# The second image joins the shared silu group, and the planner gets a new table of ties

## The chip, the cores and the metric

The kernel runs on one core of a Trainium2 chip. The metric is the device time of one execution in microseconds (us). An execution with a profiler attached also gives a trace of every instruction; times inside it are counted from the first instruction of the program. The engines are named PE (matrix multiply), PEld (its weight loads), DVE (vector), ACT (scalar activations), POOL (GpSimd) and SP (the queue that issues the DMAs).

## The reference, cut to what matters

The input is eight images of 384 channels and 1024 positions in float32. For every image a selective-scan mixer is applied and added to the input; for the first five images a quantised feed-forward network follows.

```python
t = layernorm(layernorm_over_channels(x))        # per position
xm, z = split(t @ in_proj_w.T)                   # 768 + 768 channels
xc = silu(causal_conv3(xm) + conv_b)
dt, Bm, Cm = split(xc @ x_proj_w.T)              # 24 + 16 + 16
dt = softplus(dt @ dt_proj_w.T + dt_proj_b)
h[l] = exp(dt[l] * A) * h[l-1] + dt[l] * xc[l] * Bm[l]   # 16 states a channel
y = (sum over states of h[l] * Cm[l] + xc * D) * silu(z)
x = x + mlp(y @ out_proj_w.T)                    # gelu between two layers, then its residual
# images 0 to 4 only: t = t + ffn(layernorm(t)), signs as weights, clipped by a maximum over the image
```

## The kernel before, in words

**Tiling.** An image is worked on in two halves of 512 positions (`T`). A tile is 128 partitions wide; 768 channels are six such groups, kept in three pieces of two groups each (`PER` = 2). Four kinds of work exist for an image `b`:

- the *front* (`s1`, L697): two norms, the products `p_in` and `p_z` with `in_proj_w` (six groups each, three 128x128 weights a group; each float32 multiply appears as two matmul records in the trace), the convolution on DVE (L763), silu of `xc`, the product `p_dbc` (L797), a fold and a row sum `p_all` (L807), the products `p_dt` (L828), softplus of `dt`, and the product `dtx` = dt·xc on POOL (L844). Results go to DRAM: `xc_d`, `z_d`, `dt_d`, `dtx_d` and `rows_d`;
- the *scan* (`s2`, L862, and `scan`, L875): twelve units an image. Each loads its rows again, spread out over states, and runs through exp on ACT (`da`, L584), multiplications on POOL (L992), the scan instruction on DVE (L1017) and sums on PE into `py` (L956). Image 0 and image 7 are scanned half by half, the others whole;
- the *back* (`s3`, L1051): the products `p_out`, `p_h` and `p_o` with gelu between them;
- the *feed-forward* (`ffn`, L1255) of images 0 to 4, with the products `p_y`.

**Order.** No loop order of the program is the order of the instructions. `Plan.add` (L218) writes down every operation with its engine, an assumed cost and what it reads and writes. `Plan.run` (L265) then plays these out on an assumed clock and emits the instructions of each engine in the order in which the planner starts them. On the chip each engine keeps that order and waits for semaphores. When an engine has several operations that could start, `choose` (L291) narrows the set and `rank` (L316) sorts it: scans of images first by class, fronts (lanes 1, 4, 11, 14) next, everything else after that. Within a class the order is the order of writing down, `op.prio[2]`, moved by up to 16 places either way by a hash, `turned` (L100). The seed of this hash comes from the table `TURNS` (L93): entry n is used while the planner's clock is between 100·n and 100·(n+1) us. Bits above 65535 of an entry change a rule for that stretch, such as fronts later or scans first on DVE. Past the end of the table the seed is 0, which leaves the written order. The planner also emits a small multiply called `spare` (L478), of which nothing is used, where it expects PE to be idle for over 0.7 us.

**Buffers.** Tiles come from rings, which hand out buffers in the order of writing down within a lane. Fronts use the ring `front` (six pieces) and the weight ring `w_f` (four). The front of image 1 alone runs in lane 11 and takes other rings: `hid` (nine pieces) for `xc`, `dt` and `z`, and `w_b` (three weights); both serve the back and the feed-forward later. PSUM has three buffers `mm` and two `da`.

**The activation tables.** An ACT operation carries the name of the table that it needs (`silu`, `softplus`, `gelu`, `exp`, or none). `choose` stays with the present table, where it is not exp, while an operation of it can start. `in_place` (L713) makes a group of silu or softplus, one instruction per piece: the first instruction waits for all the pieces of the group, the rest follow it.

```python
        def in_place(func, table, *ts):                                   # L713
            parts = [t[k] for t in ts for k in range(KD)]
            for p, piece in enumerate(piece for t in ts for piece in t.pieces):
                mine = parts[p * PER : (p + 1) * PER]
                self.act(..., r=parts if p == 0 else mine, w=mine, table=table)
...
            z = gate(half, t) if b in JOINT else None                     # L783
            in_place(AF.Silu, "silu", *([xc, z] if z else [xc]))
            by_pair("xc", half, xc)
            if z:
                by_pair("z", half, z)
...
            if not z:                                                     # L857, after softplus, dtx and dt
                z = gate(half, t)
                in_place(AF.Silu, "silu", z)
                by_pair("z", half, z)
```

`gate` (L733) writes down the six weight loads, the six `p_z` groups and their copies; `by_pair` (L704) the stores to DRAM.

Of the kernel before, what the change touches and what calls it, by code (L numbers as in the profile page):

```python
# [34 lines left out]
B, C, L = 8, 384, 1024  # L35
# [36 lines left out]
MM = 0.859  # L72
MODE = 0.097
SWITCH = 0.22
JOINT = range(2, B)
BATCH = 2
SIGNAL = 0.05
DRAIN = 0.2
# [12 lines left out]
STRETCH, REACH = 100, 16  # L91
LATE_FRONTS, DVE_SCANS, POOL_SCANS, ACT_STAGES = 1 << 16, 1 << 17, 1 << 18, 1 << 19
TURNS = (  # L93
    59965, 29935, 54697, 25830, 41556, 52704, 5806, 54013, 24204, 552223,
    25982, 47623, 34875, 16007, 24111, 42172, 43083, 15421, 638691, 11540,
    33479, 220645, 233617, 13861, 59336, 49176, 14182, 227647, 59245, 317456,
)


# [318 lines left out]
class Layer:  # L418
# [278 lines left out]
    def s1(self, b):  # L697
# [15 lines left out]
# [4 lines that stand above are left out]
                self.act(lambda piece=piece: piece.real, lambda piece=piece: piece.real, func,  # L717
                         c_act(PER * T), r=parts if p == 0 else mine, w=mine, table=table)
# [14 lines left out]
        def gate(half, t):  # L733
            z = self.split(r_z, KD, "z")
            for m in range(KD):
                w = self.weights(r_w, KC, a["in_proj_w"][KD + m])
                pm = self.mm3(w, t, [t[k] for k in range(KC)], [z.pieces[m // PER]], "p_z")
                self.affine(
                    lambda m=m, z=z: z.at(m), lambda pm=pm: pm.real, [pm], [z[m]]
                )  # L740
            return z

        for half, cols in enumerate(HALVES):
# [38 lines left out]
            all_m = [xc[m] for m in range(KD)]  # L782
            z = gate(half, t) if b in JOINT else None  # L783
            in_place(AF.Silu, "silu", *([xc, z] if z else [xc]))
# [647 lines left out]
```

## Time and profile before

| What | Value |
|---|---|
| time, median of 3 runs | 3134.88 us (3129.45 to 3136.87) |
| time of the profiled execution | 3132.08 us |
| its span, first to last instruction | 3130.3 us |
| mean granted PE clock | 0.993 |
| PE busy | 3049.4 us (97%), of it 58.6 us in `spare` |
| POOL busy | 2802.1 us (90%) |
| DVE busy | 2599.5 us (83%) |
| ACT busy | 2019.1 us (65%), of it 273.3 us in 213 table loads |
| DMA | 751.76 MB, 240 GB/s on average |

Busy times are unions of the instructions of an engine. A matmul record is longer (597 ns) than the distance from one to the next, since they are pipelined; so the idle time of PE says more than its busy time does. Line numbers are those of the kernel before. Many operations are recorded by a helper, so L568 (all large products) and L584 (all table functions) are told apart by the tiles' names.

### The profile page before, as it was taken

To read this page: it belongs to the slowest core of one execution; us is meant where nothing else is said; L and a number is where in the kernel's file an instruction comes from. 1 tells how busy PE (TensorE), PEld (TensorE's weight loads), DVE (VectorE), ACT (ScalarE), POOL (GpSimd) and SP (SyncE) were. 2 spreads that over 40 slices of the span, in tenths; PEclk is the share of its full clock that TensorE was granted. 3 is DMA by queue.
4 is the path that set the end of the run, shared out by engine and by line. 5 is a ranking of instruction groups with operands and counts; after the bars stand their busy time and mean duration, and the time that the engine had idled before them with its cause. 6 is when DMAs were issued, how large, how long until landed. Compare 5 with 4: busy or idle time off the path is not lost.

```text
span 3130.3 us, 32297 instructions
## 1 busy us (share of the span) xinstructions
PE 3049.4 (97%) x10202; PEld 1243.8 (40%) x10202; DVE 2599.5 (83%) x2053; ACT 2019.1 (65%) x2406; POOL 2802.1 (90%) x1095
## 2 busy tenths in 40 slices
PE   9899999999999999999999999999999999999999
PEld 4334333333333444434343334343334444333334
DVE  4787888999987889878799888898788988798880
ACT  4887787776576566667666665666745556666562
POOL 2889888999999998999989998999999999999880
PEclk9999999999999999999999999999999999999999
DMA  7999778777787667777679675886877756756442
GB/s 231 305 312 314 241 255 282 272 251 254 256 318 241 207 202 259 280 263 259 202 256 319 206 231 194 298 276 211 269 250 229 238 187 220 243 187 211 155 152 73
DMA packets 348969, 751.76 MB, mean 240 GB/s; under 512 B 36480, under 2 KB 113792, under 8 KB 339584
## 3 DMA queue, kind: packets, MB, share of 16 engines
q1 hardware_dynamic: 348368, 749.61, 71.9%
q8 instruction: 82, 1.34, 0.2%
q14 instruction: 87, 0.71, 0.1%
q10 hardware_dynamic: 432, 0.09, 0.0%
HBM read 569.21 MB, written 180.36 MB: 239 GB/s over the span
## 4 chain that ended last, share of the span: by engine, by line
PE 53%; DVE 6%; DMA 5%; ACT 5%; POOL 4%; issue 2%; SPq 0%; DVEq 0%; POOLq 0%; ACTq 0%
PE p_y L568 16%; PE p_o L568 11%; PE p_h L568 9%; PE py L956 7%; PE p_out L568 5%; POOL u L992 3%; DVE u L1017 2%; PE p_in L568 2%; DVE da L1017 2%; PE p_z L568 2%; ACT da L584 1%; ACT L584 1%; DMA w_b<-in_mlp_w 1%; DMA w<-in_mlp_w 1%; DMA w_n<-bin_w 1%
## 5 line engine op out<-in xcount | busy, mean ns | idle before, releaser
L584 ACT ACTIVATE da<-dt_r,a_neg 128x1024 f32<-128x1024 f32 (+1 forms) x960 | 898.2, 944 | 559.4 <-DVE u L1017 292.1
L992 POOL TENSOR_TENSOR u<-dtx_r,bc 128x2048 f32<-128x2048 f32 (+1 forms) x360 | 1186.4, 3311 | 75.7 <-PE py L956 38.8
L1017 DVE TENSOR_TENSOR_SCAN u<-da,u 128x1024 f32<-128x1024 f32 (+1 forms) x436 | 871.2, 2009 | 165.7 <-POOL u L992 77.7
L992 POOL TENSOR_TENSOR u<-u,bc 128x2048 f32<-128x2048 f32 (+1 forms) x274 | 900.0, 3290 | 74.4 <-DVE u L1017 68.0
L568 PE MATMUL p_h<-t,w_b 128*128 128x512 f32 x1152 | 513.1, 597 | 10.7 <-DMA w_b<-in_mlp_w 5.0
L568 PE MATMUL p_o<-g,w 128*128 128x512 f32 x1152 | 512.3, 597 | 7.5 <-DMA w<-in_mlp_w 5.7
L1017 DVE TENSOR_TENSOR_SCAN da<-da,dtx_r 128x1024 f32<-128x1024 f32 (+1 forms) x192 | 380.4, 2014 | 51.1 <-POOL dtx_r L992 31.4
L992 POOL TENSOR_TENSOR dtx_r<-dtx_r,bc 128x2048 f32<-128x2048 f32 (+1 forms) x120 | 397.0, 3312 | 1.8
L568 PEld LDWEIGHTS p_o<-g,w 128*128 128x128 f32 x1152 | 214.6, 190 | 299.7 <-issue 271.1
L568 PE MATMUL p_y<-gf,w_n 128*128 128x512 f32 x720 | 323.5, 601 | 9.3 <-DMA w_n<-bin_w 6.0
L568 PEld LDWEIGHTS p_h<-t,w_b 128*128 128x128 f32 x1152 | 213.9, 190 | 298.1 <-issue 259.8
L568 PE MATMUL p_y<-tn,w_b 128*128 128x512 f32 x720 | 318.9, 597 | 3.2 <-DVE rstd L685 2.5
L956 PE MATMUL py<-u,fold 128*32 128x512 f32 x2304 | 303.2, 625 | 0.0
L1017 DVE TENSOR_TENSOR_SCAN da<-da,u 128x1024 f32<-128x1024 f32 (+1 forms) x140 | 280.8, 2037 | 11.7 <-ACT da L584 10.8
L584 ACT ACT_TABLE_LOAD x213 | 273.3, 1283 | 5.5 <-DMA dt_r<-dt_d 1.8
L568 PE MATMUL p_out<-yg,w 128*128 128x512 f32 x552 | 245.5, 596 | 2.1 <-DMA w<-in_out_proj_w 1.3
L568 PE MATMUL p_in<-t,w_f 128*128 128x512 f32 x504 | 230.6, 606 | 12.6 <-issue 5.2
L568 PE MATMUL p_z<-t,w_f 128*128 128x512 f32 x504 | 227.1, 599 | 2.0 <-issue 1.0
L568 PEld LDWEIGHTS p_y<-gf,w_n 128*128 128x128 f32 x720 | 134.1, 191 | 196.0 <-issue 173.4
L568 PEld LDWEIGHTS p_y<-tn,w_b 128*128 128x128 f32 x720 | 134.4, 190 | 184.5 <-issue 167.0
L1037 DVE TENSOR_TENSOR dtx_r<-da,bc 128x1024 f32<-128x1024 f32 x144 | 170.8, 1214 | 0.1
L599 ACT ACTIVATE g<-p_h,v_vecs 128x512 f32<-128x512 f32 x159 | 107.5, 678 | 89.9 <-PE p_h L568 89.4
(131 smaller groups left out, 3152.4 us busy)
## 6 DMA issues: line engine op xcount, KB each, us to landing
dtx_r<-dtx_d SPq DMA_DIRECT2D x72, 1024.0 KB, 5.9
dt_r<-dt_d SPq DMA_DIRECT2D x144, 512.0 KB, 5.1
w_b<-in_mlp_w SPq DMA_DIRECT2D x192, 192.0 KB, 3.5
w<-in_mlp_w SPq DMA_DIRECT2D x96, 384.0 KB, 3.4
w_f<-in_in_proj_w SPq DMA_DIRECT2D x168, 192.0 KB, 4.4
y_d<-y SPq DMA_DIRECT2D x120, 256.0 KB, 4.9
gf<-y_d SPq DMA_DIRECT2D x60, 512.0 KB, 6.3
xc_d<-xc SPq DMA_DIRECT2D x48, 512.0 KB, 6.1
```

Source lines behind the costliest of these rows:

```text
L568: self.nc.tensor.matmul(p.real, w.real[:, w0 + k, :], t.at(k0 + k), start=start and k == 0, stop=stop and k == n - 1,)
L584: lambda: self.nc.scalar.activation(out(), in_(), func, **{k: v() if callable(v) else v for k, v in kw.items()}),
L599: nc.scalar.activation(out(), in_(), AF.Identity, bias=bias, scale=scale)
L956: nc.tensor.matmul(py.real[g * DQ : (g + 1) * DQ, :], self.fold, hc, start=False, stop=(q == NQUAD - 1), skip_group_check=True,)
L992: nc.gpsimd.tensor_mul(u.real[:, x], t.real[:, x], row.real.unsqueeze(2).to_broadcast([P, n, 2]))
L1017: da=da, in_u=in_u: nc.vector.tensor_tensor_scan(to(i), da.real[:, i, :], in_u(i), state.real[:, col : col + 1] if half else 0.0, ALU.mult ...
L1037: nc.vector.tensor_mul(u.real[:, 0, :, t], da.real[:, 0, :], cq.real)
```

## The change

`JOINT` is the set of images whose front makes `z` before the silu of `xc`, so that one group of six silu instructions serves both. It was images 2 to 7 and becomes images 1 to 7. For both halves of image 1, the six weight loads, the six `p_z` groups with their copies, three silu instructions and three stores of `z` are written down ahead of `p_dbc`, and no longer after `dt`. The rings of image 1 (`hid` and `w_b`) stay. The table `TURNS` is another one throughout, with 31 entries for 30, and with other entries that carry rule bits; so the order among equals can differ in any part of the kernel. No operation is added or left out.

```diff
-JOINT = range(2, B)
+JOINT = range(1, B)
...
 TURNS = (
-    59965, 29935, 54697, 25830, 41556, 52704, 5806, 54013, 24204, 552223,
-    25982, 47623, 34875, 16007, 24111, 42172, 43083, 15421, 638691, 11540,
-    33479, 220645, 233617, 13861, 59336, 49176, 14182, 227647, 59245, 317456,
+    49843, 0, 14285, 9398, 319468, 15448, 107859, 44413, 48398, 70601,
+    17958, 35163, 36370, 107033, 276429, 33905, 16527, 550033, 11076, 25285,
+    28427, 1340, 188371, 35681, 649167, 22066, 0, 682652, 12089, 9636,
+    42095,
 )
```

## The prediction

> **What bounds the kernel.** I read the page first, then busy times by stretch, then the timelines of PE and ACT where PE is not full. By stretch (busy us and instruction count per engine, granted clock, DMA share, GB/s):
>
> ```profile
> 0.00:100.00 100.00, 88.47 (x353) 44.15 (x354) 45.99 (x71) 52.03 (x70) 36.86 (x35) 0.97 0.75 251
> 100.00:320.00 220.00, 207.25 (x773) 87.32 (x772) 177.13 (x182) 185.55 (x277) 193.36 (x135) 0.95 0.92 304
> 320.00:3046.00 2726.00, 2673.06 (x8880) 1077.39 (x8879) 2368.45 (x1792) 1765.87 (x2041) 2571.91 (x926) 1.00 0.72 240
> 3046.00:3131.00 85.00, 80.59 (x200) 34.97 (x198) 7.92 (x10) 15.70 (x20) 0.00 (x0) 1.00 0.25 75
> ```
>
> The columns after the length are PE, PEld, DVE, ACT, POOL. From 320 us on PE is 98% busy and POOL 94%. Part of PE's time is `spare`, which is disguised idling: the same view for that tile gives 11.22, 22.46, 24.29 and 0.60 us (sum 58.57). So PE lacks real work for 100-88.5+11.2 = 22.8 us, then 220-207.25+22.46 = 35.2 us, 77.2 us, and about 4 us. Every other microsecond is product work that the change leaves alone. **The end is set by PE: its fixed work plus these holes.** The second bound is the scan, seen in the end of PE's timeline:
>
> ```profile
> 3051.00 1.11 PE L956 MATMUL py<-u,fold 128*32 128x512 f32 x8
> 3051.93 1.08 PE L956 MATMUL py<-dtx_r,fold 128*32 128x512 f32 x8
> 3052.93 4.56 PE L568 MATMUL p_out<-yg,w 128*128 128x512 f32 x10
> ...
> 3064.63 31.06 PE L568 MATMUL p_h<-t,w_b 128*128 128x512 f32 x72
> 3095.53 31.06 PE L568 MATMUL p_o<-g,w 128*128 128x512 f32 x72
> ```
>
> The last sums of the scan end at 3053, and PE then has about 8.7 us of `p_out` that does not need them (3052.93 to 3061.62). So the scan has some 8 us to spare at the end, and no more: **to end earlier by much, both must be quicker; to end later, one is enough.**
>
> The change acts in 95 to 330 us, where image 1's front lies. There ACT shows 26 table loads. This is `z` of image 1, half 1, as a separate group, and the joint group of image 2, half 0:
>
> ```profile
> 262.32 1.28 ACT L584 ACT_TABLE_LOAD   x1
> 263.61 1.06 ACT L584 ACTIVATE z<-z 128x1024 f32<-128x1024 f32 x1
> ...
> 267.54 1.28 ACT L584 ACT_TABLE_LOAD   x1
> ```
>
> ```profile
> 283.09 1.28 ACT L584 ACT_TABLE_LOAD   x1
> 284.38 1.06 ACT L584 ACTIVATE xc<-xc 128x1024 f32<-128x1024 f32 x1
> 285.46 1.28 ACT L584 ACT_TABLE_LOAD   x1
> ...
> 292.11 1.28 ACT L584 ACT_TABLE_LOAD   x1
> 293.40 2.00 ACT L584 ACTIVATE z<-z 128x1024 f32<-128x1024 f32 x2
> ```
>
> The joint group is **torn in two**: one silu, then back to exp, then the rest with a second pair of loads. Over the whole trace 29 loads lead to silu; 8 belong to the four halves of images 0 and 1, so 21 serve the 12 joint halves, 1.75 each against 2 for a half with two groups. And PE pays for the wait:
>
> ```profile
> 291.81 5.16 PE L478 MATMUL spare<-small 128*128 128x256 f32 x22
> 296.89 1.07 PE L797 MATMUL p_dbc<-xc,w_f 128*64 128x512 f32 x2
> ```
>
> **What the Trainium skill says.** "ScalarE: Activation LUTs", section "What ACT_TABLE_LOAD costs", gives about 1283 ns for a load and about 1380 ns of drain. The trace agrees on the first (1283 mean, 213 loads) and not on the second: the copy before 262.32 ends at 262.30, and silu starts at 263.61. I price a load at 1.29 us. The same page's "Table sets: the hidden batching unit" says to batch by set; the torn groups show that a wider group saves less than a pair of loads here. "Perfetto Trace Analysis", section "Identifying the Most-Contended Engine", warns that matmul busy time misleads; the 58.6 us of `spare` inside 97% agree. "TensorE: Matmul & The Clock Gate", Part 1, says that PE's clock halves after idle windows; 0.95 in 100 to 320 against 1.00 after it (about 11 us) agrees.
>
> **The change part by part.** The sum is against the profiled 3132.08 us (span 3130.3 plus 1.8 around it), 2.8 below the median of 3134.88; I move the sum to the median.
>
> *Table loads.* Two separate groups become one in each of two halves: at best four loads, 4 x 1.29 = 5.2 us of ACT; at worst none, if both are torn; at the 1.75 of the others, one load, 1.3 us. This comes back only where someone waits for ACT: in 95 to 330 us DVE waits 17.0+10.8 us for `da` and POOL 6.6 us for `dt`, 34.4 of 235 us, 15%. I take -0.2 us, with ends -5.2 and 0.
>
> *`p_z` ahead of `p_dbc`.* Per half, 36 records (six per 2.8 us in the timeline, hence 15.6 us of PE), six copies (0.58 us on ACT or 0.69 on DVE), three silu (1.05 us), six weight DMAs (192 KB) and three `z_d` stores move forward. On SP's queue they pass the loads for `p_dbc` and `p_dt`, one `rows_d`, three `dtx_d` and three `dt_d` issues; all these, softplus on ACT, and the three `dtx` products on POOL (2.37 us each) come about 15.6+3.1 = 19 us later. In POOL's order the multiplications of image 0's scan stand behind `dtx`; a late `dtx` would hold them. What covers the delay of the data: image 1's scan begins at its first `py` of about 546 us (the 13th unit), while its `dt` is stored by 240. If that cover were gone, 19 us per half would count. The `hid` ring takes 3+3+3 = 9 pieces, exactly its size, as before: cost 0, at worst one wait for a store to land (6.6 us median).
>
> *PE's waits in this stretch.* `p_z` of image 1 now waits for its weights (1.59 and 2.47 us), since `w_b` hands them out behind those of `p_dt`; that goes: -4.1. In exchange both `p_dbc` come behind a joint group, like image 2's (5.2 us of `spare`), where half 1 now has 5.0 us and half 0 none: +5.4. Net +1.3. Lower end: neither hole forms, -9.1. Upper end: the whole stretch of 281 to 297 us around image 2's group, 13.1 us of `spare`, comes twice in place of the 5.0: +21.2.
>
> *The table of ties.* It removes no work, and no row of before shows its effect. What the order among equals can do is read from images with equal work: in the stretches 899, 1269, 1639 and 1995 (each to the next, the last to 2365) PE lacks work for 4.8, 8.1, 3.1 and 6.7 us, but in 2365 to 2696 for 331-327.45+19.39 = 22.9, with a hole around the maximum of a feed-forward (2502 to 2516, filled with `spare`). One such hole more or less is about 18 us. I take 0, with ends -20 and +25; the gain is the shorter side because of the scan.
>
> *Sum:* -0.2+1.3+0 = +1.1 on 3134.9, so 3136.
>
> **The rivals.**
> 1. *Little moves* (chance 0.38): the sum above, 3136, own range 3122 to 3150. For it: the gain lies on ACT, which is 65% busy, and 300 us ahead of need.
> 2. *Slower* (0.32): the joint stage of image 1 repeats image 2's hole. PE has nothing else in hand at 100 to 320, since no back or feed-forward is ready before 360. 2 x 13.1 - 5.0 = 21.2, so 3156. It decides from the point where `spare` and idle of PE in 100 to 320 exceed 35.2 us and the scan doesn't gain the difference. Against it: image 0's second half can fill in, as `p_in` does at 97 to 113.
> 3. *Faster* (0.26): the new order has no hole like that at 2502 (-18) and all four loads go (-5.2): 3112. For it: such holes are 20 us of 139. Against it: the scan would have to end over 8 us earlier too, with POOL at 94%.
> 4. *The change doesn't do what it says* (0.04): both groups of image 1 are torn, 213 loads stay, and the order changes only among idle neighbours: 3135.
>
> **How the numbers follow.** A measurement of this kernel tells 0.3%, 9.4 us, from no change: 3125.5 and 3144.3 are the borders. Rival 1 gives 0.05 faster, 0.22 same, 0.11 slower; 2 gives 0.32 slower; 3 gives 0.26 faster; 4 gives 0.01, 0.02, 0.01. Together 0.32, 0.24, 0.44. Cases of both signs hold most of the chance, so the range reaches to both: from 3104 (rival 3 with most of its ends) to 3170 (rival 2 with 14 us of the table's upper end). The predicted time is rival 1's.
>
> **What would show it.** Right: 209 to 213 table loads; `p_z<-t,w_b` ahead of `p_dbc<-xc,w_b` in both halves, with no wait for weights; `spare` of 17 to 28 us in 100 to 320; the thirteenth `py` within 10 us of 546; PE idle after 320 within 15 us of 77. Wrong: a change of over 10 us that is already there when image 1's scan starts (rival 2's place), or one that arises in a single image after 900 us (the table, with either sign), or a last scan sum that comes over 8 us late relative to PE's end.

## The result, and the profile after

The changed kernel takes 3143.01 us (median of 10 runs, 3139.17 to 3150.51), the kernel before 3133.16 us beside it (10 runs, 3127.42 to 3139.77). The ratio is 1.0031, with a 95% interval of 1.0019 to 1.0042: slower by some 10 us. The profiled execution took 3139.18 us, with a span of 3137.3, which is 7.0 more than the one of before; the stretches below are to be held against these 7.0. All line numbers of the changed kernel are higher by one.

Busy times by stretch, the changed kernel (after the length: PE, PEld, DVE, ACT, POOL, each with its count, then granted clock, DMA share, GB/s):

```profile
0.00:100.00 100.00, 91.58 (x352) 44.71 (x353) 46.44 (x67) 47.56 (x68) 37.09 (x35) 0.98 0.72 238
100.00:320.00 220.00, 199.46 (x711) 80.04 (x709) 180.62 (x192) 189.31 (x271) 189.93 (x135) 0.91 0.91 299
320.00:2240.00 1920.00, 1894.28 (x6413) 768.74 (x6414) 1700.77 (x1272) 1264.04 (x1441) 1805.42 (x610) 1.00 0.76 254
2240.00:3046.00 806.00, 783.72 (x2530) 321.54 (x2529) 671.87 (x517) 478.35 (x584) 752.88 (x306) 1.00 0.64 207
```

The same view of the kernel before, for the last two of these stretches:

```profile
320.00:2240.00 1920.00, 1882.57 (x6339) 755.32 (x6338) 1688.01 (x1259) 1279.44 (x1449) 1808.34 (x613) 1.00 0.75 252
2240.00:3046.00 806.00, 790.49 (x2542) 322.07 (x2541) 680.44 (x534) 486.43 (x593) 763.57 (x314) 1.00 0.66 211
```

Add the time of `spare` (after: 13.19, 8.67, 18.64 and 26.98 us; before: 11.22, 22.46, 3.70 and 20.59) and PE lacks real work as follows:

| Stretch (us) | before | after | difference |
|---|---|---|---|
| 0 to 100 | 22.8 | 21.6 | -1.2 |
| 100 to 320 | 35.2 | 29.2 | -6.0 |
| 320 to 2240 | 41.1 | 44.4 | +3.3 |
| 2240 to 3046 | 36.1 | 49.3 | **+13.2** |

The four rows sum to +9.3, and from 3046 us to the end both kernels lack some 4.5 us. PE's busy time without `spare` is 2.4 us shorter after (2988.4 against 2990.8), which leaves about the 7.0.

In 100 to 320 the granted clock fell from 0.95 to 0.91 at the same time, which gives back about 0.04 x 220 = 9 us at most; so image 1's front, where the joint group acts, comes out near level. The largest loss is in the last 800 us, where image 1 is long done. The scan shows when it arises. An image is scanned in twelve units, and a unit starts with ACT's `py<-xr,v_vecs`. The first unit of an image starts, before and after, at 545.8 and 538.8 us (image 1), 899.1 and 901.5 (image 2), 1994.9 and 1992.2 (image 5), 2364.6 and 2363.7 (image 6), 2695.7 and 2709.9 (image 7). **At the start of image 6 the two kernels are level; image 6 takes 346 us in place of 331.**

Level is a balance. Image 1's own scan takes 362.7 us in place of 353.3, which uses up its earlier start. The profiles of the experiments that keep the first 22 entries agree (363 to 365 us with the group and the early entries of the change, 353 with those of before); the cause is open. The earlier start itself is less sure: a profile shows one execution, and in six profiles with the same order up to here image 1's scan starts between 534.7 and 546.5 us.

The end of PE's timeline, the changed kernel:

```profile
3061.81 1.12 PE L957 MATMUL py<-u,fold 128*32 128x512 f32 x8
3062.75 1.08 PE L957 MATMUL py<-dtx_r,fold 128*32 128x512 f32 x8
3063.76 5.42 PE L569 MATMUL p_out<-yg,w_n 128*128 128x512 f32 x12
...
3071.57 31.17 PE L569 MATMUL p_h<-t,w_b 128*128 128x512 f32 x72 [0.24 <-ACT t L598]
3102.58 31.06 PE L569 MATMUL p_o<-g,w 128*128 128x512 f32 x72
```

The last sums of the scan end at 3063.8 against 3053.0, 10.8 us late. After them PE had 8.7 us of independent `p_out` before and 5.3 us now; the closing `p_h` begins at 3071.57 against 3064.63, 6.9 us late, and the span is 7.0 us longer. What POOL did meanwhile, in image 6's stretch and from there to the last sum, before and then after:

```profile
2364.00:2696.00 332.00, 328.45 (x1105) 138.57 (x1104) 301.06 (x207) 188.46 (x199) 321.56 (x95) 1.00 0.67 217
2696.00:3053.00 357.00, 348.88 (x1077) 138.33 (x1075) 291.52 (x268) 223.59 (x316) 323.75 (x183) 1.00 0.59 184
```

```profile
2364.00:2710.00 346.00, 340.32 (x1149) 146.26 (x1148) 299.80 (x210) 188.52 (x203) 333.86 (x105) 1.00 0.67 219
2710.00:3064.00 354.00, 339.17 (x1048) 133.34 (x1047) 294.19 (x265) 213.92 (x304) 312.10 (x173) 1.00 0.56 174
```

In image 6's stretch POOL is idle for 10.4 us before and for 12.1 after. Of the 14 us more, 12.3 are more work, and 10.4 of these are the end of image 4's feed-forward (the clip of `y` and six additions), which the kernel before runs after image 6, at 2701 to 2721 us. So image 6's longer scan is for the most part work that was moved into it. After it POOL has 11.7 us less to do, and the stretch is only 3 us shorter: POOL is idle for 33.3 us before and for 41.9 after. Both stretches together have 10.3 us more of idle time, about the delay of the scan. It is a fitting reading, and not shown, that this work costs time in image 6, where POOL is 97% busy, and hides after it, where POOL is 91% busy in the kernel before: no run moved these operations alone, and e8 below speaks against POOL's work alone as the bound of image 6.

The growth of POOL's idle time is in waits for a scan of DVE, and after image 6 (5.2 us before and 6.4 after in image 6's stretch). From there to 3046 us (engine, line, what it waited for: us in total, times, longest), before and after:

```profile
POOL u L992 <- DVE u L1017: 11.6, 10, 3.2
```

```profile
POOL u L993 <- DVE u L1018: 22.0, 12, 7.6
```

One example shows what order does. At 2605.7 us POOL of the changed kernel turns to the end of image 4's feed-forward, ahead of the product `dtx_r` that DVE's next scan needs. (On POOL and DVE the classes of the order are not the whole rule: there `choose`, L309, lets any other operation that is ready go ahead of the scan's, unless the bits of the table's entry say otherwise.) Then comes DVE's own line:

```profile
2605.70 2.90 POOL L1322 TENSOR_SCALAR y<-y 128x1536 f32<-128x1536 f32 x2
2608.56 4.97 POOL L1330 TENSOR_TENSOR x<-x,y 128x512 f32<-128x512 f32 x4
2613.49 4.06 POOL L993 TENSOR_TENSOR dtx_r<-dtx_r,bc 128x2048 f32<-128x2048 f32 x1
```

```profile
2617.59 4.48 DVE L1018 TENSOR_TENSOR_SCAN da<-da,dtx_r 128x1024 f32<-128x1024 f32 x2 [11.20 <-DMA x<-mid_d]
```

DVE stands still for 11.2 us, the longest of its gaps in this part. The releaser named in the bracket is the one inferred; the scan reads `dtx_r`, and it begins 0.04 us after that product ends (2617.55). The kernel before does the same clip and additions at 2701 to 2721, with a gap of DVE of 9.3 us at 2716, so this hole is an example of how order costs, not the whole sum.

### The profile page after: what moved, and what is told of

Its sections match the earlier page's. It is cut to its first block, busy times and chain, and to the rows that moved or that the text cites. A ratio compares the mean times of both kernels' runs of the same rounds, so it can differ in the third digit from the quotient of the medians.

```text
span 3137.3 us, 32358 instructions
## 1 busy us (share of the span) xinstructions
PE 3056.4 (97%) x10228; PEld 1252.1 (40%) x10228; DVE 2617.0 (83%) x2064; ACT 1999.0 (64%) x2387; POOL 2791.9 (89%) x1086
## 4 chain that ended last, share of the span: by engine, by line
PE 65%; DVE 9%; POOL 8%; DMA 8%; ACT 6%; issue 3%; SPq 0%; DVEq 0%; POOLq 0%; ACTq 0%
PE p_y L569 15%; PE p_o L569 12%; PE p_h L569 11%; PE py L957 8%; POOL u L993 6%; PE p_in L569 6%; PE p_out L569 5%; PE p_z L569 5%; DVE u L1018 4%; DVE da L1018 2%; ACT da L585 2%; ACT L585 1%; DMA w_b<-in_mlp_w 1%; POOL dtx_r L993 1%; PE p_dt L829 1%
## 5 line engine op out<-in xcount | busy, mean ns | idle before, releaser
L569 PE MATMUL p_o<-g,w 128*128 128x512 f32 x1152 | 513.3, 598 | 11.3 <-DMA w<-in_mlp_w 10.4
L1018 DVE TENSOR_TENSOR_SCAN da<-da,u 128x1024 f32<-128x1024 f32 (+1 forms) x140 | 282.8, 2040 | 15.5 <-POOL u L993 10.3
L585 ACT ACT_TABLE_LOAD x201 | 257.9, 1283 | 8.5 <-DMA dt_r<-dt_d 5.1
L600 ACT ACTIVATE y<-p_y,v_vecs 128x512 f32<-128x512 f32 x140 | 95.2, 681 | 110.8 <-PE p_y L569 91.4
```

Source lines behind the costliest of these rows:

```text
L569: self.nc.tensor.matmul(p.real, w.real[:, w0 + k, :], t.at(k0 + k), start=start and k == 0, stop=stop and k == n - 1,)
L585: lambda: self.nc.scalar.activation(out(), in_(), func, **{k: v() if callable(v) else v for k, v in kw.items()}),
L600: nc.scalar.activation(out(), in_(), AF.Identity, bias=bias, scale=scale)
L1018: da=da, in_u=in_u: nc.vector.tensor_tensor_scan(to(i), da.real[:, i, :], in_u(i), state.real[:, col : col + 1] if half else 0.0, ALU.mult ...
```

## The experiments

The theories named in them: A, a table of ties only suits the list of operations that it was made for, and the entries for the late part lose the 10 us; B, the joint group costs them early; C, the new table costs them and the old one would still serve. Ratios are to the kernel before in the same session.

**One part at a time: group and table.** Four kernels, with two lines changed:

```diff
 e1: -JOINT = range(2, B)   +JOINT = range(1, B)      (old table)
 e2: -JOINT = range(1, B)   +JOINT = range(2, B)      (new table)
 e3: JOINT = range(1, B)    +TURNS = ()
 e4: JOINT = range(2, B)    +TURNS = ()
```

> Image 1 joins the shared silu group, with the table of ties of the kernel before. Theory A (a table only suits the list of operations that it was made for, and the joint group as such is worth little): well over the kernel before, 3160 to 3200 us, since the hash moves other operations once the numbering of image 1's operations changes. Theory B (the joint group costs the 10 us by itself, the table is neutral): 3140 to 3148 us. Theory C (the new table costs it, the joint group is neutral, the old table still works): 3130 to 3137 us.

> Image 1 keeps its two separate silu groups, with the new table of ties. Theory A: well over both kernels, 3150 to 3200 us. Theory B: the 10 us go away, 3130 to 3137 us. Theory C: the 10 us stay, 3140 to 3148 us.

> Image 1 joins the shared silu group, and the table of ties is empty: the written order among equals, no rule bits. Theory A: 3150 to 3200 us, and within 25 us of the separate groups without a table, with either sign. Theory B: 8 to 12 us over the separate groups without a table. Theory C: equal to the separate groups without a table within 5 us.

> Image 1 keeps its two separate silu groups, and the table of ties is empty. Theory A: 3150 to 3200 us; the distance from the kernel before is what a fitted table is worth. Theories B and C: the table is a small correction, 3135 to 3150 us.

| Groups of image 1 | old table | new table | no table |
|---|---|---|---|
| separate | 3133.03 (the kernel before) | 3232.29, ratio 1.0323 (1.0304 to 1.0341) | 3201.24, 1.0225 (1.0206 to 1.0244) |
| joint | 3238.05, 1.0337 (1.0314 to 1.0361) | 3143.01, 1.0031 (1.0019 to 1.0042) | 3246.56, 1.0368 (1.0344 to 1.0393) |

C is out. Theory A's first half holds, by more than it had asked for: a table is worth 68 us to the list that it was made for (3201 to 3133; for the joint list 3247 to 3143, 104 us), and on the other list it does about as well as no table, or worse (3232 against 3201). All four times lie above the ranges that A gave. So the change cannot be taken apart into a group and a table: each was measured at about +100 us alone, together they are +10. The 45 us between the two kernels without a table are one order against another, and none of the theories had asked for so much; whether the group as such has a share in them is left open.

**Cut late.** The same two kernels with their first 22 entries only:

```diff
-TURNS = (49843, 0, ... 42095)      # 31 entries; 30 in the kernel before
+TURNS = (... the first 22 of them)
```

> The changed kernel with only the first 22 entries of its table; from the planner's 2200 us on (about 2240 us on the chip, image 6 not begun) the written order holds. Theory A (the loss of the change is in the late entries, which suit their order less well than those of before do): 3145 to 3165 us, and within 6 us of the kernel before cut at the same place. Theory B (the joint group itself costs it, early): at least 8 us over the kernel before cut at the same place.

> The kernel before with only the first 22 entries of its table. Theory A: 3148 to 3165 us, so that the late entries of before are worth 15 to 30 us and those of the changed kernel about 10 us less. Theory B: the late entries are worth the same in both kernels, and this one stays 8 us or more under the changed kernel cut at the same place.

Measured: the changed kernel cut 3144.97 us, ratio 1.0045 (1.0035 to 1.0055); the kernel before cut 3158.18 us, 1.0084 (1.0057 to 1.0111). **Cut at the same place the joint kernel is the quicker one, by 13 us.** B, which asked for at least 8 us the other way, is out. The late entries of before are worth 3158.2-3131.7 = 26 us; those of the change some 4 us by the ratios (1.0045-1.0031), whose intervals overlap. A's direction holds; its "within 6 us" does not. The 13 us do not come from the early part: in the two profiles image 7's scan starts at 2709.7 us (joint) and 2708.7 (separate), and the spans end at 3139.5 and 3147.9.

**Other late entries.** Both kernels again with their first 22 entries, and others after them, out of some 4000 draws each (the 60000 of the expectation is a slip; no run shows either count), ranked by the planner's own clock:

```diff
 before: -233617, 13861, ... (8 late entries)  +53134, 57054, 17476, 180164, 262144, 22707, 57774, 0, 30260, 27246
 after:  -188371, 35681, ... (9 late entries)  +25178, 28433, 57189, 164963, 36420, 61776, 2219, 0, 296835, 0
```

> The kernel before with its first 22 entries kept and other entries after them (60000 other draws of hash seeds and rule bits, chosen by the planner's own clock). If the late entries decide by luck of the draw (theory A): between the kernel before and its cut version, 3133 to 3150 us. If the late entries of before were nothing special (theory B, the joint group costs the 10 us early): within 4 us of the kernel before.

> The changed kernel with its first 22 entries kept and other entries after them, drawn in the same way and with the same effort. Theory A: the draw can go either way, 3135 to 3150 us; below 3137 would show that nothing in the joint group stands against the time of before. Theory B: 3141 us or more, since the loss is already there.

Measured: separate groups 3143.16 us, ratio 1.0037 (1.0025 to 1.0049); joint groups 3134.35 us, 1.0015 (1.0007 to 1.0024). **With other late entries the order of the two is reversed**: the joint kernel comes within 0.15% of the kernel before, and the separate one, without the change, is as slow as the change was. The joint one's interval overlaps with that of the changed kernel (1.0019 to 1.0042), so that it gained on it is likely and not shown. At the place of the example above, POOL of the joint one has `dtx_r` ahead of the clip:

```profile
2604.26 4.07 POOL L988 TENSOR_TENSOR dtx_r<-dtx_r,bc 128x2048 f32<-128x2048 f32 x1
...
2618.45 2.93 POOL L1317 TENSOR_SCALAR y<-y 128x1536 f32<-128x1536 f32 x2 [2.04 <-ACT y L580]
```

while the separate one has the clip and the additions ahead of it again, and a gap of DVE of 14.0 us at 2620. That this is a reason for the difference is not shown. The profiled execution of the joint one took 3142.5 us, 8.1 over its median, and in it image 6 takes 348.9 us and the last sum ends at 3067.6; in the separate one these are 349.6 and 3067.5.

What the profiles do show is that the kernel before is the exception. Image 6 takes 352.2 us (changed kernel, cut), 349.3 (before, cut), 348.9 and 349.6 (joint and separate with other late entries) and 346.2 in the changed kernel, against 331.1 before; and of these only the kernel before has the end of image 4's feed-forward after image 6 on POOL. None of these kernels beats the one before.

**What bounds the late part.** The order of the changed kernel is kept, and work is left out where the instructions are emitted, so that the outputs differ:

```diff
 e7, p_h of image 5 only:   -for k in range(n):            +for k in range(1):
 e8, image 6, states 0-3:   -tensor_mul(u, u, C rows)      +tensor_mul on half the columns
 e12: both
```

> The changed kernel, same order, but of the product p_h of image 5 only the first of three weights is multiplied in (48 of 72 multiplies, 41 us of PE work, are left out, at 2590 to 2725 us). If PE's work sets the end in this part: 25 to 41 us less than the changed kernel's 3143 (3102 to 3118). If the scan sets it: at most 8 us less (3135 to 3143).

> The changed kernel, same order, but one of the POOL products of image 6 (the second one of the first four states, u times the C rows) is made on half the columns: 24 instructions of about 4.1 us become about 2.1 us, 47 us of POOL work left out, at 2364 to 2710 us. If the scan's POOL work sets the end: 25 to 45 us less than the changed kernel's 3143 (3098 to 3118). If PE's work sets it: at most 8 us less.

> The changed kernel, same order, with both of the earlier cuts at once: two thirds of p_h of image 5 left out on PE (41 us of work) and half of one POOL product of image 6 (12 instructions, about 24 us of work). Alone they gave 3 us and nothing. If PE and POOL bound this stretch together, each hiding what the other gains: 15 to 24 us less than the changed kernel's 3143, so 3119 to 3128. If the fixed order of the queues holds it (loads of weights that are issued behind other transfers, DVE at its place in the round): at most 8 us less, 3135 or more.

Measured: e7 3137.26 us, ratio 1.0020 (1.0010 to 1.0030); e8 3140.82 us, 1.0030 (1.0020 to 1.0039); e12 3135.26 us, 1.0012 (1.0004 to 1.0021). The expectation of e8 had its dose wrong: image 6 is scanned whole, so there are 12 instructions and not 24. The busy time of these lines in image 6, the changed kernel and e8 (length, POOL busy and count):

```profile
2364.00:2710.00 346.00, 305.18 (x79) 1.00 0.67 219
```

```profile
2375.00:2722.00 347.00, 281.48 (x79) 1.00 0.66 218
```

So 23.7 us of POOL's work went, and image 6 still took 347 us: in it POOL's waits for DVE's scans rose from 6.4 to 14.5 us, and those for PE's sums from 4.8 to 14.5. On PE 41 us went and the ratio fell by 0.0011, 3 us; both cuts together gave 0.0019, 6 us, less than the 15 that a joint bound of PE and POOL would have given. All these intervals overlap with that of the changed kernel, so the gains are small and not sure. PE's waits in 2580 to 2740 us in e7 say where most of its 41 us went:

```profile
PE p_h L573 <- DMA w_b<-in_mlp_w: 25.7, 8, 6.2
```

It is 1.8 us in the changed kernel. The products ran out of weights, whose loads stand in SP's queue behind transfers with waits of their own: there SP waits 20.7 us for PE's `p_o`, 14.3 for ACT's `da` and 14.2 for `p_h` itself. The rest went to the clock: the granted clock in this stretch is 0.88 in place of 1.00, and PE's busy time falls from 156.97 to 129.95 us, by 27 and not by 41. So neither PE's work nor POOL's sets the end of this part by itself. What is left is the fixed order of the queues with the waits in it, DVE's work, which was not cut, and in e7 the clock; which of them binds was not separated.

**Table loads.** The order of the changed kernel, with identity in place of silu in every image, so silu is left out of the computation:

```diff
-    func,
+    AF.Identity if func == AF.Silu else func,
```

> The changed kernel, same order, but all silu instructions of all images take the identity function, which needs no table: the computation is changed in that silu is left out. About 52 table loads of 1.28 us go, 67 us of ACT work. If ACT's table loads were on the path: 20 us or more less than the changed kernel's 3143. My step (15% of ACT time comes back): about 10 us less, 3133. If loads are covered in full: within 4 us of 3143.

The row of table loads in the page of this kernel:

```profile
L585 ACT ACT_TABLE_LOAD x151 | 193.7, 1283 | 6.7 <-DMA dt_r<-dt_d 4.1
```

50 loads fewer than the 201 of the changed kernel, 257.9-193.7 = 64 us of ACT. Measured: 3141.41 us, ratio 1.0033 (1.0023 to 1.0043), against 1.0031 no change that these intervals can tell. The loads of silu's table are covered.

## Why the prediction was right or wrong

**Sign and size.** 3136 was predicted, with 3104 to 3170 and a chance of 0.44 on slower, the largest of the three; 3143.0 was measured, inside the range and inside the 3122 to 3150 of the likeliest case. The reason that the text gave for the longer side towards slower, that a later end of the scan is enough, is what happened (+10.8 us of the scan, +7.0 of the end). But the mechanism that rival 2 named did not occur, and the likeliest case had the wrong term at nothing. So the number is in part luck: the range is 66 us wide, PE's lack in the front fell by 6 us where +1.3 was summed, and the late part added what the sum had at 0. Of the five signs of being right two came (`p_z` ahead of `p_dbc` without a wait for weights; the scan's start within 10 us of 546), and three did not: 201 loads for 209 to 213, 8.7 us of `spare` in 100 to 320 for 17 to 28, and 93.7 us of PE's lack from 320 to 3046 us for 77 within 15.

**Table loads** (-0.2 us; 209 to 213 loads): the count was 201. Image 1 gave one pair, as at a rate between whole and torn: half 0 came whole, half 1 torn. ACT's timeline, half 0 and then half 1:

```profile
134.96 1.28 ACT L585 ACT_TABLE_LOAD   x1
...
139.59 2.94 ACT L585 ACTIVATE z<-z 128x1024 f32<-128x1024 f32 x3
```

```profile
236.78 1.28 ACT L585 ACT_TABLE_LOAD   x1
238.07 1.06 ACT L585 ACTIVATE xc<-xc 128x1024 f32<-128x1024 f32 x1
239.15 1.28 ACT L585 ACT_TABLE_LOAD   x1
...
242.98 1.28 ACT L585 ACT_TABLE_LOAD   x1
```

The other ten loads went elsewhere, through the order (45 loads led to gelu before, 40 after). The share of 15% that was to come back was too high: 64 us of loads were worth nothing that could be measured.

**PE's waits for the weights of `p_z`** (-4.1): right, no `p_z` waits for a load in that stretch any more; one `p_in` does, for 1.38 us.

**`p_dbc` behind the joint group** (+5.4, the end +21 being rival 2): wrong; neither hole forms, the lower end that the text gave. In half 1 `p_z` of image 2 fills the time, and no `spare` stands ahead:

```profile
238.64 10.57 PE L569 MATMUL p_z<-t,w_f 128*128 128x512 f32 x24
249.14 1.11 PE L957 MATMUL py<-u,fold 128*32 128x512 f32 x8
250.07 1.08 PE L957 MATMUL py<-dtx_r,fold 128*32 128x512 f32 x8
251.08 2.79 PE L798 MATMUL p_dbc<-xc,w_b 128*64 128x512 f32 x12
```

The statement that PE has nothing else in hand before 360 us was the slip in it: other fronts are in hand. A hole of the same size arose in another place, 8.5 us from 291.7 us on, where PE waited for the squares (`sq`) of a norm of a later image.

**`p_z`, its stores and the later `dt`** (cost 0, cover of 300 us): right; image 1's scan began at 538.8, no later than before.

**The table** (0, ends -20 and +25): the term that was mis-sized. From 2240 us on, far from the front, PE's lack grew by 13 us and the last sum came 10.8 us late; the bounds held, and the sign to look for was named (a change that arises in one image after 900 us). But the new entries did not add a hole to a neutral order: with its late entries cut or redrawn the kernel before itself loses 26 and 12 us (1.0084 and 1.0037), and its image 6 takes 349 and 350 us in place of 331. What the text missed is how far a table carries: it read the effect of order from holes of single images, some 20 us, where the runs without a table gave 68 and 104.

**"The end is set by PE: its fixed work plus these holes":** true as a sum, not as a cause. Taking 41 us out of the fixed work made the holes larger and the clock lower; it brought 3 us.

## What to carry to other kernels

Where the order of several in-order queues is fixed ahead, a table of ties can belong to one exact list of operations, as it did here: compare two versions each with its own table, and expect part of the difference to be the draw. Look for the place where two traces part (here image 6's scan, from 2364 us) before a reason is sought in the edit itself, and hold both against traces of other draws: here they show that the kernel before was the exception. Ask, too, whether a longer stretch holds lost time or moved work. And test a bound by leaving work out in the same order: an engine that is 98% busy and whose work can go without the end moving does not set the end by itself.

## What the runs showed of the hardware that was not expected

Fifty table loads, 64 us of an engine that is 64% busy, changed the time by nothing that could be measured (ratio 1.0033 against 1.0031). With two thirds of `p_h` of image 5 left out, the granted PE clock in 2580 to 2740 us fell from 1.00 to 0.88 (0.76 in 2600 to 2620, where PE was busy for 13.06 of 20 us), and two records of `p_h` that take 1.02 us at 2591 take 2.05 at 2615. So part of the work that went was paid back as a slower clock on the rest: an estimate from these numbers is 41-27 = 14 us.
